# Pace of the linear steps in an AdaLN transformer block: which half's attention three MLP steps are counted to

## The chip, the cores and the metric

The kernel runs on one core of a Trainium2 chip. The metric is the device time of one execution in microseconds (us). A core has five engines that run side by side and meet through semaphores: TensorE (PE, with its weight loads as PEld), VectorE (DVE), ScalarE (ACT), GpSimd (POOL) and SyncE (SP), which here issues nearly all DMAs.

## The reference

Eight sequences of 1024 tokens with 512 features go through one transformer block whose normalisations are modulated by a condition (float32 throughout):

```python
mod = silu(condition) @ Wada + bada                  # shift, scale and gate, twice
sh_a, sc_a, gt_a, sh_m, sc_m, gt_m = split(mod, 6, axis=1)
xm = layernorm(x, g1, be1) * (1 + sc_a) + sh_a
q, k, v = split_heads(xm @ Wqkv)                     # 16 heads of 32
s = where(causal, q @ k.T * 32**-0.5, -inf)
x = x + gt_a * (softmax(s) @ v @ Wproj + bproj)
xm = layernorm(x, g2, be2) * (1 + sc_m) + sh_m
x = x + gt_m * (gelu(xm @ W1 + b1) @ W2 + b2)        # 512 -> 2048 -> 512, exact gelu
```

## The kernel before, in words

**Blocks and halves.** The work is cut into 16 blocks of 512 tokens, two to a sequence: `blocks = [(b, h)]`, `NB = 16`. Block n is a first half (h = 0, n even) or a second half (h = 1, n odd). A first half attends only to its own tokens; a second half attends to the first half's keys as well.

**Two streams on one engine.** `attend()` (L1699) walks through the attention of blocks 0 to 15 in order. `linear()` is a generator that yields before each matmul of the linear steps. Both feed TensorE, and Python decides at build time in which order their instructions are written, by a small model of when each engine is free (`now`, `written`, `left`).

**Attention.** Heads come in four groups g of four heads. A second half has four whole key tiles more per group than a first half. Each unit goes: `weights_T` (L1547) subtracts the row maxima and multiplies q and k into the PSUM tile `st`, ACT takes the exponential of the scores (L1583) into `pT`; `close` (L1754) multiplies an earlier `pT` with v (L1611); POOL adds up the weights (L1696). A first half has 10 units and so 10 exponentials, a second half 26. The row maxima come from score units (`scores`, L1477) worked out one group ahead in the same PSUM tile, of which there is one; DVE masks them (L1491) and reduces them (L1494), `split_maxima` (L1499) cuts the maximum into three bf16 parts (`mcols`, last instruction L1516), and `maxima_rows` (L1524) turns these into rows by matmuls (L1532) that ACT copies out (L1538).

**Linear steps.** The linear stream is a list of steps per window: window w is what is counted to the attention of block w. The steps are `k`, `q`, `v` (projections), `proj` (output projection), `at` and `mt` (transposes with modulation, L657), `u` (a quarter of the first MLP product with its gelu, L1031) and `d` (a part of the second MLP product), with small ones for loads, norms and gate rows. Most are written in Strassen's form: seven products on quarters of the operands. All of their matmuls are issued by the helper `matmul` (L201) at line 205. One call of it is 8 matmul instructions in the trace. A `k`, `q`, `v`, `u` step is 28 calls, and the eight MLP steps of a block (`m` = u0 to u3, d0 to d3) are 4 x 28 calls and 32, 32, 16 and 32 calls. Weights come in 256 KB pieces through a ring of nine buffers, in the order of the steps.

Window w holds, for the MLP, the steps of block n = w - 1. What doesn't fit is put into the list `late`, with which the next window begins (L256):

```python
steps = late + [("v", w), ("load_xr", n)] + rows_a + [("proj", n), ("k", w + 1)]
steps += [("mt", n), ("q", w + 1)] + rows_m + own        # own: u0, u1, u2 and loads
```

In the last attention window, w = 15, only the first late step stands ahead of the loads and the projection (L251):

```python
steps = late[:1] + [("load_xr", n)] + rows_a + [("proj", n), ("mt", n)] + late[1:]
```

**The pace.** `planned_time(w)` (L327) adds up fixed costs of a window's steps (853 ns for two calls). `exp_need` (L1782) and `score_need` (L1786) give fixed costs to the attention's units. For each block, `attend` sets a rate (L1721), and each unit adds to what is due (`pace`, L1780):

```python
stream["rate"] = planned_time(n) / mine * (0.7 if n == 0 else 1.0)
stream["due"] += ns * stream["rate"]
```

`step_aside` (L1338) runs before each attention instruction group and decides whether linear work goes first; `own` and `other` are the modelled waits of the attention and of the linear stream, and `done_linear` is what the linear stream has booked (430 ns for a call):

```python
if done_linear[0] < stream["due"]:
    if other > own + 100:
        break
elif own <= max(other, 50):
    break
work()
```

So a linear stream behind its account is worked off even where the attention is ready; one that is ahead only fills the attention's waits. Apart from that, `until(condition)` (L1334) runs linear work alone: `close` calls it until v of the block whose keys come next is done. `run_excursions(1)` (L1729) hands one waiting ACT job, such as a gelu or a norm, to ACT after each exponential, and in first halves also after each score unit; it is also called for all jobs when no linear step can go on.

Of the kernel before, what the change touches and what calls it, by code (L numbers as in the profile page):

```python
# [22 lines left out]
def kernel(  # L23
# [207 lines left out]
    def mlp_steps(n):  # L231
        return [("u", n, i) for i in range(NQ)] + [("d", n, part) for part in range(4)]
# [8 lines left out]
    late = []  # L241
    for w in range(1, NB):
        n = w - 1
        m = mlp_steps(n)
        even = blocks[n][1] == 0
        rows_a = [("rows", blocks[n][0], "a")] if even else []
        rows_m = [("rows", blocks[n][0], "m")] if even else []
        own = m[:1] + ([("load_xa", w + 2)] if w + 2 < NB else []) + m[1:3]
        own += [("norm_a", w + 2)] if w + 2 < NB else []
        if w == NB - 1:  # L250
            steps = late[:1] + [("load_xr", n)] + rows_a + [("proj", n), ("mt", n)] + late[1:]  # L251
            steps += [("v", w)] + rows_m + own + m[3:6]
            late = m[6:]
        else:

            steps = late + [("v", w), ("load_xr", n)] + rows_a + [("proj", n), ("k", w + 1)]  # L256
            if w == 1:
                steps = [("load_xr", n)] + rows_a + [("k", w + 1), ("proj", n)]
            steps += [("mt", n), ("q", w + 1)] + rows_m + own
            at = [("at", w + 2)] if w + 2 < NB else []  # L260
            if blocks[w][1] == 0:

                steps += m[3:5]
                late = m[5:6] + at + m[6:]
            else:
                steps += m[3:6] + at
                late = m[6:]
        plan[w] = steps
# [104 lines left out]
    at, r0 = [], 0  # L373
# [1497 lines left out]
```

## Time and profile before

| | |
|---|---|
| median of 3 runs | 3552.7 us (3548.19 to 3553.39) |
| profiled execution: time | 3555.04 us |
| profiled execution: span | 3553.2 us |
| mean granted TensorE clock | 0.998 |
| instructions | 123721 |
| DMA traffic | 441.76 MB, mean 124 GB/s |

The span is the time from the first to the last instruction of the profiled execution; its whole time is 1.8 us longer. In the profile, L205 is line 205 of the kernel; a group such as "bank<-w,hT" names the tile written and the tiles read. Busy times are in us, the mean of one instruction in ns, and a wait is shown with the instruction that ended it. The tiles tell the linear steps apart: `hT` stands for the d steps, `xm_m` and `t_m` for the u steps, `xm_a` and `t_a` for q, k and v.

### The profile page before, as it was taken

How to read it: one execution, taken by the hardware profiler on the slowest of the kernel's cores; microseconds unless marked ns; L12 is line 12 of the kernel's file. 1: busy time of each engine (PE TensorE's matmuls, PEld its weight loads, DVE VectorE, ACT ScalarE, POOL GpSimd, SP SyncE). 2: the span in 40 equal slices, each digit the busy share in tenths (PEclk: the TensorE clock that was granted, in tenths of full speed). 3: DMA queues.
4: the chain of work that ended last, by engine and by line, in shares of the span. 5: the costliest groups of instructions: out<-in, count | busy, mean ns of one | idle time of the engine just before them, and what ended most of it. 6: DMA issues, size and time to landing. Idle time of an engine off the chain costs nothing.

```text
span 3553.2 us, 123721 instructions
## 1 busy us (share of the span) xinstructions
PE 3486.2 (98%) x56189; PEld 1814.8 (51%) x56189; DVE 1926.9 (54%) x2106; ACT 1271.1 (36%) x1407; POOL 2066.2 (58%) x2194
## 2 busy tenths in 40 slices
PE   8999999999999999999999999999999999999999
PEld 4444555445554455545555445454554545545445
DVE  5765664644636456364464645636446464554463
ACT  2335233342333524235242342423524244241521
POOL 3675745666466663666636666466664666644650
PEclk9999999999999999999999999999999999999999
DMA  6742334334343344433434334343343433435334
GB/s 209 257 147 88 115 114 119 116 107 141 116 135 108 97 138 117 147 96 97 141 111 147 99 95 140 108 150 100 94 144 106 150 96 103 133 99 152 88 115 137
DMA packets 319944, 441.76 MB, mean 124 GB/s; under 512 B 26568, under 2 KB 188676, under 8 KB 319420
## 3 DMA queue, kind: packets, MB, share of 16 engines
q1 hardware_dynamic: 319168, 433.54, 40.4%
q8 instruction: 443, 7.26, 0.9%
q14 instruction: 81, 0.66, 0.1%
q10 hardware_dynamic: 252, 0.29, 0.0%
HBM read 404.32 MB, written 29.41 MB: 122 GB/s over the span
## 4 chain that ended last, share of the span: by engine, by line
PE 87%; DVE 5%; ACT 3%; POOL 2%; issue 1%; DMA 1%; SPq 0%; DVEq 0%; ACTq 0%; POOLq 0%
PE bank L205 60%; PE sc L1477 8%; PE po L1611 7%; PE st L1570 6%; DVE mx L1494 3%; PE st L1558 2%; PE bank L657 2%; PE bank L1632 2%; ACT pT L1583 1%; POOL pT L1696 1%; DVE sc L1491 1%; DVE hT L1089 1%; DVE xr L162 1%; ACT hT L1031 1%; PE bank L1532 0%
## 5 line engine op out<-in xcount | busy, mean ns | idle before, releaser
L1696 POOL TENSOR_TENSOR pT<-pT,pT 128x256 f32<-128x256 f32 (+3 forms) x1254 | 1200.0, 992 | 260.2 <-ACT pT L1583 165.3
L1583 ACT ACTIVATE pT<-st 128x2048 f32<-128x2048 f32 x288 | 541.0, 1878 | 1154.6 <-PE st L1570 1048.6
L205 PE MATMUL bank<-w,hT 128*32 128x256 f32 x14336 | 807.4, 380 | 0.3 <-ACT xm_a L667 0.2
L1494 DVE TENSOR_REDUCE mx<-sc 128x4 f32<-128x2048 f32 (+3 forms) x384 | 665.7, 1754 | 134.0 <-PE sc L1477 126.5
L205 PEld LDWEIGHTS bank<-w,hT 128*32 128x32 f32 x14336 | 455.2, 110 | 343.6 <-issue 49.5
L205 PE MATMUL bank<-xm_m,w 128*32 128x256 f32 x8192 | 502.1, 381 | 1.8 <-DVE u_u L197 1.7
L205 PE MATMUL bank<-t_m,w 128*32 128x256 f32 x6144 | 380.7, 380 | 0.4 <-DVE hT L197 0.3
L205 PEld LDWEIGHTS bank<-xm_m,w 128*32 128x32 f32 x8192 | 254.6, 110 | 245.1 <-issue 81.2
L1588 POOL TENSOR_SCALAR_AFFINE_SELECT pT<-pT 128x512 f32<-128x512 f32 x256 | 168.8, 677 | 344.2 <-ACT pT L1583 342.8
L1477 PE MATMUL sc<-kT,qT 32*128 32x512 f32 (+3 forms) x3072 | 329.2, 520 | 6.0 <-DVE mx L1494 2.9
L1491 DVE TENSOR_TENSOR sc<-sc,mask 128x1024 f32<-128x1024 f32 (+1 forms) x160 | 162.9, 1018 | 277.1 <-PE sc L1477 186.7
L1611 PE MATMUL po<-pT,v 128*32 128x512 f32 (+3 forms) x3072 | 305.9, 493 | 2.8 <-POOL pT L1588 2.8
L1570 PE MATMUL st<-qT,kT 32*128 32x512 f32 (+3 forms) x3072 | 300.2, 486 | 0.0
L205 PEld LDWEIGHTS bank<-t_m,w 128*32 128x32 f32 x6144 | 192.7, 110 | 168.4 <-issue 32.5
L205 PE MATMUL bank<-xm_a,w 128*32 128x256 f32 x3968 | 245.5, 381 | 0.0
L165 POOL TENSOR_TENSOR qT<-top,rec 128x512 f32<-128x512 f32 x61 | 78.2, 1282 | 274.5 <-ACT rec L1650 270.9
L1477 PEld LDWEIGHTS sc<-kT,qT 32*128 32x128 f32 x3072 | 129.7, 184 | 161.6 <-ACT pT L1583 75.3
L197 DVE TENSOR_TENSOR hT<-bank,u_u 128x512 f32<-128x512 f32 x192 | 128.4, 686 | 134.0 <-PE bank L205 131.5
L205 PE MATMUL bank<-w,qT 128*32 128x256 f32 (+1 forms) x2944 | 190.4, 399 | 0.8 <-DMA w<-in_L_cond_Wproj_dram 0.8
L1031 ACT ACTIVATE hT<-hT,cols 128x512 f32<-128x512 f32 x256 | 164.2, 711 | 54.9 <-DVE hT L197 54.3
L205 PE MATMUL bank<-t_a,w 128*32 128x256 f32 x2944 | 182.8, 380 | 0.9 <-DMA w<-kept_qkv_S 0.9
L205 PEld LDWEIGHTS bank<-xm_a,w 128*32 128x32 f32 x3968 | 125.6, 110 | 105.4 <-issue 22.5
(217 smaller groups left out, 3491.9 us busy)
## 6 DMA issues: line engine op xcount, KB each, us to landing
w<-in_L_cond_W_dram SPq DMA_DIRECT2D x384, 256.0 KB
w<-kept_up_S SPq DMA_DIRECT2D x256, 256.0 KB
w<-kept_down_S SPq DMA_DIRECT2D x256, 256.0 KB
w<-kept_qkv_S SPq DMA_DIRECT2D x180, 256.0 KB
w<-in_L_cond_Wqkv_dram SPq DMA_DIRECT2D x147, 256.0 KB
hat<-in_x_dram SPq DMA_DIRECT2D x64, 256.0 KB
xr<-in_x_dram SPq DMA_DIRECT2D x64, 256.0 KB
out_dram<-xr SPq DMA_DIRECT2D x64, 256.0 KB
```

The source lines that it names most:

```text
L165: nc.gpsimd.tensor_tensor(out, a, b, op)
L197: nc.vector.tensor_tensor(out, src, other, op)
L205: nc.tensor.matmul(ps[r, :], lhsT[:, r], rhs, start=start, stop=stop, skip_group_check=True)
L1031: nc.scalar.activation(hT[:, i, :], hT[:, i, :], AF.Gelu, bias=cols[:, O_B1 + f : O_B1 + f + 1])
L1477: nc.tensor.matmul(sc[:, j, c0 : c0 + w], qTs[n][r, gg, ts(qt, P)], keys_of(n, kh)[r, gg, :w], start=True, stop=True, skip_group_check=True,)
L1491: nc.vector.tensor_tensor(place, place, shape_of.to_broadcast(place.shape), ALU.add)
L1494: nc.vector.tensor_reduce(maxima[n, gg][:, kh, qt, :], sc[:, :, c0 : c0 + w], axis=AX.X, op=ALU.max)
L1570: nc.tensor.matmul(st[:, j, c0 : c0 + w], kT[r, gg, ts(k % NTT, P)], qT[r, gg, TB - w :], start=False, stop=True, skip_group_check=True,)
L1583: nc.scalar.activation(pT[:, :, :used], st[:, :, :used], AF.Exp, scale=scale)
L1588: nc.gpsimd.affine_select(diagonal, diagonal, pattern=[[0, HPG], [1, P]], compare_op=ALU.is_ge, fill=0.0, base=0, channel_multiplier=-1,)
L1611: nc.tensor.matmul(po[r, TB - w :], v[:, k % NTT, g * P + j * hd : g * P + (j + 1) * hd], pT[:, j, c0 : c0 + w], start=(k == 0), stop=last ...
L1696: nc.gpsimd.tensor_tensor(into, into, pT[:, j, c0 : c0 + w], ALU.add)
```

## The change

For a window w that is a first half, the lists before and after are:

```diff
             at = [("at", w + 2)] if w + 2 < NB else []
             if blocks[w][1] == 0:
 
-                steps += m[3:5]
-                late = m[5:6] + at + m[6:]
+                late = m[3:6] + at + m[6:]
             else:
                 steps += m[3:6] + at
                 late = m[6:]
```

Before, u3 and d0 end the list of a first half's window and d1 opens that of the second half's. After, u3, d0 and d1 all open that of the second half's. This concerns the first halves 2, 4, ..., 14 and the second halves 3, 5, ..., 15 behind them. The order of the linear stream stays the same except in window 15, where `late[:1]` is u3 instead of d1, so that `load_xr`, the gate rows, `proj` and `mt` of block 14 come between u3 and d0 instead of between d1 and d2. No instruction's work is added or taken away.

## The prediction

> **What bounds the kernel now.** I read the page first. It gives the span, TensorE's (PE) busy time and the number of exponentials.
>
> ```profile
> span 3553.2 us, 123721 instructions
> ...
> PE 3486.2 (98%) x56189; PEld 1814.8 (51%) x56189; DVE 1926.9 (54%) x2106; ACT 1271.1 (36%) x1407; POOL 2066.2 (58%) x2194
> ...
> L1583 ACT ACTIVATE pT<-st 128x2048 f32<-128x2048 f32 x288 | 541.0, 1878 | 1154.6 <-PE st L1570 1048.6
> ```
>
> PE is idle for 3553.2 - 3486.2 = 67.0 us, and no other engine is near its limit. The change adds no instruction, so its worth is what it does to those 67 us. The 288 exponentials are 8 x (10 + 26): a first half has 10 units, a second half 26. Counting them in the timeline gives each attention's stretch ("window n" runs from the first exponential of half n to that of the next). The busy time by windows, for 4 and 12 (first halves) and 5 and 13 (second halves): start:end, length, PE busy (instructions), then PEld, DVE, ACT, POOL, clock, DMA.
>
> ```profile
> 807.50:982.70 175.20, 175.00 (x2932) 95.56 (x2928) 101.52 (x114) 55.01 (x67) 92.48 (x109) 1.00 0.43 128
> 982.70:1242.50 259.80, 256.13 (x4036) 129.87 (x4032) 130.20 (x138) 103.15 (x108) 170.87 (x169) 1.00 0.38 114
> ...
> 2553.60:2722.00 168.40, 166.56 (x2773) 89.93 (x2769) 96.14 (x107) 51.41 (x62) 90.57 (x109) 1.00 0.42 124
> 2722.00:2991.70 269.70, 265.85 (x4212) 135.47 (x4208) 133.88 (x146) 108.88 (x116) 169.18 (x170) 1.00 0.38 116
> ```
>
> Idle PE is 0.2 and 3.7 us in windows 4 and 5, 1.8 and 3.9 us in 12 and 13. The list of waits says on what: the first row is window 12's, the second stands in window 5's answer and, digit for digit, in 13's.
>
> ```profile
> PE bank L1532 <- POOL mcols L1516: 1.5, 1, 1.5
> ...
> PE st L1558 <- DVE mx L1494: 3.1, 4, 1.1
> ```
>
> **The change, part by part.** Outside window 15 the order of the linear steps stays the same: what leaves a first half's list leads the next one. Only the rates differ. By the code's own costs a first half needs 65.2 us (exponentials 15.0, scores 50.2) and a second half 100.6 us. The planned linear time goes from 131.4 to 105.8 us and from 162.1 to 187.7 us: (14 + 16) x 853 ns = 25.6 us move, u3 and d0. The third step named, d1, was counted late already. The rates go from 2.02 to 1.62 and from 1.61 to 1.87.
>
> The rate acts only where the linear account is behind what is due. Elsewhere linear work just fills the wait for the score tile, and at v(w), which every attention needs early, it runs alone until v is done (a burst). So I counted the linear matmuls (line 205) by stretch; 8 instructions are one call. The rows are: the last but one and the last unit of window 4; the last of 12; the last two of 14; the first five units of 5; the burst in 5; that in 13; three units of 13 with one score group each; two units of 15 with none.
>
> ```profile
> 928.30:958.10 29.80, 22.54 (x396) 12.43 (x400) 1.00 0.47 143
> 958.10:982.70 24.60, 18.97 (x340) 10.55 (x336) 1.00 0.40 113
> ...
> 2702.80:2722.00 19.20, 13.56 (x237) 7.16 (x233) 1.00 0.29 86
> 3114.90:3140.80 25.90, 18.66 (x324) 10.08 (x328) 1.00 0.35 104
> 3140.80:3157.80 17.00, 11.36 (x196) 5.84 (x192) 1.00 0.33 94
> ...
> 982.70:1025.80 43.10, 29.47 (x516) 15.87 (x512) 1.00 0.35 101
> ...
> 1025.80:1067.70 41.90, 37.53 (x688) 21.99 (x680) 1.00 0.58 181
> 2765.50:2816.80 51.30, 46.97 (x864) 27.72 (x856) 1.00 0.56 174
> ...
> 2899.70:2925.10 25.40, 16.52 (x285) 8.98 (x289) 1.00 0.42 136
> 3157.80:3167.30 9.50, 4.69 (x84) 2.36 (x80) 1.00 0.27 79
> ```
>
> The last unit has 42.5 calls in window 4, 29.6 in 12 and 24.5 in 14. It shrinks because the account books 430 ns for a call that the plan counts at 426.5; over the 672 calls of a pair of windows that is 2.4 us. I take 24.5 as what the score tile's waits absorb unforced, so by window 14 the account holds almost nothing. With 25.6 us (60 calls) less due, every first half falls to that level: window 4 gives up (340 - 196 + 396 - 324) / 8 = 27 calls, window 12 gives up 5, window 14 none. In the next second half the account is then ahead, so its first five units fall from 64.5 calls to the unforced (285 + 84) / 8 = 46, 18 fewer. The burst makes up for both: in window 5 from 86 calls to 86 + 27 + 18 = 131, in window 13 from 108 to 108 + 5 + 18 = 131. From there the linear position, the attention unit and who waits for whom are as before, and at the end of the second half the sums due are equal.
>
> So 18 to 45 calls move later by some tens of us, in seven pairs of windows. They cost nothing themselves if PE stays full in the longer burst. Its cover is the linear stream alone: 48 calls in 20.93 us (0.43 us each) without an idle entry (fourth row of the next timeline). Its DMA share is 0.56 at 174 GB/s, so pieces have room. SP's queue keeps its order; POOL and DVE have fewer attention instructions in a burst.
>
> What can cost is a PE wait in the stretches that lose calls. The timelines show one: TensorE's rows of maxima (line 1532) behind POOL's split. First window 4, then window 12, the same place.
>
> ```profile
> 811.08 6.25 PE L205 MATMUL bank<-w,hT 128*32 128x256 f32 x112
> ...
> 821.56 0.41 PE L1532 MATMUL bank<-ident_b,mcols 128*32 128x128 bf16 x16
> ...
> 2557.19 4.09 PE L205 MATMUL bank<-w,hT 128*32 128x256 f32 x72
> ...
> 2564.05 0.41 PE L1532 MATMUL bank<-ident_b,mcols 128*32 128x128 bf16 x16 [1.52 <-POOL mcols L1516]
> ```
>
> With 14 calls and more after the scores nothing is late; with the unforced 9 PE stands for 1.52 us, and the linear calls and the row's copy on ACT stand behind it. In windows 4, 6 and 8 the account still forces the longer fill; at the lower rate (10.8 us due in that unit become 8.7) it does so no more. I take 3 x 1.5 = 4.5 us, with ends 0 and 4.5.
>
> The second halves have the same rows just before the burst. In window 13:
>
> ```profile
> 2757.82 6.25 PE L205 MATMUL bank<-w,hT 128*32 128x256 f32 x112
> ...
> 2765.25 2.80 PE L205 MATMUL bank<-w,hT 128*32 128x256 f32 x48
> 2767.86 0.41 PE L1532 MATMUL bank<-ident_b,mcols 128*32 128x128 bf16 x16
> ...
> 2780.32 20.93 PE L205 MATMUL bank<-w,hT 128*32 128x256 f32 x384
> ```
>
> And the split on POOL, in window 13 and in window 12, with DVE's instruction beside the latter:
>
> ```profile
> 2762.54 0.25 POOL L1515 CAST mcols<-rest 128x16 bf16<-128x16 f32 x1
> 2762.87 0.27 POOL L1516 TENSOR_TENSOR mcols<-rest,mcols 128x16 bf16<-128x16 f32 x1
> ...
> 2561.70 1.15 POOL L1515 CAST mcols<-rest 128x16 bf16<-128x16 f32 x1
> 2562.93 1.07 POOL L1516 TENSOR_TENSOR mcols<-rest,mcols 128x16 bf16<-128x16 f32 x1
> ...
> 2561.52 2.35 DVE L1089 TENSOR_TENSOR hT<-hT,hT 128x1024 f32<-128x1024 f32 x2
> ```
>
> The split ends at 2763.14, and the rows start 4.7 us later, after 14 + 6 = 20 calls. Some 9 to 11 calls fewer take 3.9 to 4.8 us: no wait, or 0.1. I take 0.2 us x 7 = 1.4 us; the ends are 0 and window 12's 1.5 each, 0 to 10.5.
>
> In window 12 the two POOL instructions took 2.2 us instead of 0.5, within a DVE subtraction that reads two SBUF tiles. The Trainium skill ("SBUF — State Buffer", section "SBUF: two separate sides") says that such a DVE operation and a POOL operation that reads SBUF hold one port pair in turn, exclusively; these rows agree. By it the split is quick or slow as the first subtraction of a d step meets it or not, which speaks against moving d0 there.
>
> In window 15 the order does change: `late[:1]` is u3 instead of d1, so load_xr(14), proj(14) and mt(14) come before d0 and d1, with load_xr's four DMAs and the gate rows' two. proj follows load_xr directly in both, and mt waits for v(15) in both: 0, from -1 to +2 us.
>
> The sum is 4.5 + 1.4 = 5.9 us. The profiled execution took 3555.0 us, span 3553.2 and 1.8 around it; it would take 3560.9. It stands 2.3 us above the median of the runs, 3552.7, on which I put the forecast: **3558.6 us**.
>
> **The rivals.**
>
> *Slower by a late gelu.* d1 needs u3's gelu, which is handed out one per exponential. Until window 15, 7028 + 5248 u instructions are 54.80 steps of 224:
>
> ```profile
> L205 PE MATMUL bank<-xm_m,w 128*32 128x256 f32 x7028 | 432.4, 381 | 1.8 <-DVE u_u L197 1.7
> ...
> L205 PE MATMUL bank<-t_m,w 128*32 128x256 f32 x5248 | 325.4, 380 | 0.4 <-DVE hT L197 0.3
> ```
>
> So 33.5 calls are left to u3's end at that unforced level, 34 to 39 with d0's interleaved, and the sixth exponential comes at call 46. The margin is some 7 calls, 3 us. If it is missed, the gelu is issued inside the burst, behind the copy that ends d0. These are the table load, gelu and copy of window 13:
>
> ```profile
> 2755.26 1.28 ACT L1031 ACT_TABLE_LOAD   x1
> 2756.55 2.56 ACT L1031 ACTIVATE hT<-hT,cols 128x512 f32<-128x512 f32 x4
> 2762.84 0.58 ACT L192 COPY p_d<-bank 128x512 f32<-128x512 f32 x1 [3.73 <-PE bank L205]
> ```
>
> PE would stand for 0.58 + 1.28 + 2.56 = 4.4 us. Near the end of the kernel a PE wait of 2.2 us is in a stretch with a clock of 0.94, which is 0.06 x 30 = 1.8 us lost:
>
> ```profile
> 3400.00:3430.00 30.00, 27.77 (x452) 13.87 (x448) 24.46 (x23) 6.38 (x9) 26.89 (x20) 0.94 0.37 116
> ...
> PE po L1611 <- POOL pT L1588: 2.2, 1, 2.2
> ```
>
> That gives 7 x (4.4 + 1.8) + 4.5 = 48 us, 3601. Chance 0.11. The Trainium skill ("TensorE: Matmul & The Clock Gate", "What's actually happening") lets the clock fall after an idle window of about 3.4 us; here 2.2 us sufficed, and 1.5 us did not (clock 1.00 in window 12). By the page the clock's part would come just the same at 4.4 us.
>
> *Slower by the rows.* If the slow split of window 12 meets the second halves' rows, 1.7 us are added to the 0.1: with a wait of 1.8 us each and the clock's 1.8 us, 7 x 3.6 + 4.5 = 30 us, 3582. It decides once the split ends 4.7 us or less after the scores' reduction than now, as fewer calls leave no slack. For it: both have the same form. Against: d0's subtraction is issued two units earlier. Chance 0.13.
>
> *Faster.* More linear work per unit could fill the 3.1 us that PE waits for DVE's maxima in a second half: 7 x 3.1 = 22 us, 3531. Against: these waits lie behind the burst, where the account is ahead, and are the same with bursts of 86 and 108 calls. Chance 0.13.
>
> *The change hardly does what it says.* Bursts reset the position and no wait appears: 3553, give or take 2. Chance 0.17.
>
> **How the numbers follow.** My forecast has 0.46, with its own range 3552 to 3566 from the ends of its terms. 0.2% is 7.1 us (3545.6 to 3559.8), about what a measurement can tell from no change. Of the forecast 0.28 lies inside, 0.18 above; of the faster rival 0.02 inside. Faster: 0.11. Same: 0.28 + 0.17 + 0.02 = 0.47. Slower: 0.18 + 0.11 + 0.13 = 0.42. The range 3543 to 3584 takes in the rows' rival and leaves out the late gelu and most of the faster case.
>
> **What would show it.** Right: first halves shorter (window 4 by about 12 us) and second halves longer by as much; bursts of about 131 calls in all second halves; a 1.5 us wait of line 1532 also in windows 4, 6 and 8; the 3.1 us unchanged. Wrong: a wait in the burst on line 1031 or 1516 above 2 us, with a clock below 1.00; or first halves as long as before.

## The result, and the profile after

| | before | after |
|---|---|---|
| median (6 runs each) | 3553.05 us (3548.19 to 3555.15) | 3527.26 us (3523.56 to 3531.16) |
| span of the profiled execution | 3553.2 us | 3524.9 us |
| idle PE (span less PE busy) | 67.0 us | 42.7 us |

The ratio is 0.9929, with a 95% interval of 0.9916 to 0.9942: 25.8 us or 0.71% faster. The forecast was 3558.6 us, so even the sign was wrong. The page after, its span, its engines and the exponentials:

```profile
span 3524.9 us, 123741 instructions
...
PE 3482.2 (99%) x56189; PEld 1800.1 (51%) x56189; DVE 1882.3 (53%) x2086; ACT 1286.5 (36%) x1422; POOL 2065.1 (59%) x2205
...
L1582 ACT ACTIVATE pT<-st 128x2048 f32<-128x2048 f32 x288 | 541.1, 1879 | 1046.0 <-PE st L1569 933.0
```

PE does the same 56189 matmuls and the same 288 exponentials follow. Of the 28.3 us that the span lost, 24.3 are idle time of PE and 4.0 its busy time. Over the twelve profiles of this case PE's busy time for these matmuls varies from 3479.3 to 3486.5 us, so the 4.0 us can't be told from chance. (The new kernel is one line shorter: its L1493 is the old L1494, its L1557 the old L1558.) Windows 4, 5, 12 and 13 after, with the columns that they had before:

```profile
797.70:964.50 166.80, 166.47 (x2772) 89.92 (x2768) 93.79 (x102) 54.14 (x65) 89.39 (x107) 1.00 0.41 126
964.50:1227.50 263.00, 262.99 (x4166) 133.61 (x4161) 130.31 (x149) 107.25 (x113) 170.38 (x171) 1.00 0.38 117
2522.80:2696.40 173.60, 172.95 (x2892) 93.77 (x2888) 94.80 (x103) 54.12 (x65) 89.53 (x109) 1.00 0.42 127
2696.40:2956.40 260.00, 259.25 (x4092) 129.97 (x4088) 130.28 (x149) 107.22 (x113) 169.85 (x170) 1.00 0.39 115
```

Window 5 had 3.7 us of idle PE and has none; window 13 had 3.9 and has 0.8. The pair 4 and 5 takes 429.8 us instead of 435.0, the pair 12 and 13 takes 433.6 instead of 438.1. From PE's list of waits (engine, tile, line, what ended the wait: total us, times, longest), first before, then after:

```profile
PE st L1558 <- DVE mx L1494: 19.1, 25, 1.1
PE bank L1532 <- POOL mcols L1516: 7.1, 6, 1.6
```

```profile
PE bank L1531 <- POOL mcols L1515: 5.1, 7, 1.6
...
PE st L1557 <- DVE mx L1493: 1.1, 2, 0.9
```

One wait explains most of it: `weights_T` waiting for DVE's maxima falls from 19.1 us in 25 waits to 1.1 us in 2. It is the 3.1 us per second half that the prediction had listed and declared unchanged; in the trace before it stands in the second halves 3 to 13 (2.4 us in window 3) and not in 15. 18.0 of the 24.3 us are this wait; the rest is spread over the maxima rows (2.0 us) and several small ones.

### The profile page after: what moved, and what is told of

Read it like the earlier page. It is cut to its first block, busy times and chain, and to the rows that moved or that the text cites. A ratio compares the mean times of both kernels' runs of the same rounds, so it can differ in the third digit from the quotient of the medians.

```text
span 3524.9 us, 123741 instructions
## 1 busy us (share of the span) xinstructions
PE 3482.2 (99%) x56189; PEld 1800.1 (51%) x56189; DVE 1882.3 (53%) x2086; ACT 1286.5 (36%) x1422; POOL 2065.1 (59%) x2205
## 4 chain that ended last, share of the span: by engine, by line
PE 93%; DVE 2%; POOL 2%; DMA 1%; issue 1%; ACT 1%; SPq 0%; DVEq 0%; POOLq 0%; ACTq 0%
PE bank L205 64%; PE sc L1476 9%; PE po L1610 7%; PE st L1569 7%; PE st L1557 2%; PE bank L656 2%; DVE mx L1493 2%; PE bank L1631 2%; POOL pT L1695 1%; PE bank L1531 0%; POOL hT L165 0%; DVE sc L1490 0%; DMA w<-in_L_cond_Wada_dram 0%; DMA hat<-in_x_dram 0%; DMA w<-in_L_cond_Wproj_dram 0%
## 5 line engine op out<-in xcount | busy, mean ns | idle before, releaser
L1695 POOL TENSOR_TENSOR pT<-pT,pT 128x256 f32<-128x256 f32 (+3 forms) x1254 | 1179.0, 975 | 202.0 <-ACT pT L1582 115.8
L205 PE MATMUL bank<-w,hT 128*32 128x256 f32 x14336 | 797.5, 379 | 0.1
L1493 DVE TENSOR_REDUCE mx<-sc 128x4 f32<-128x2048 f32 (+3 forms) x384 | 665.9, 1755 | 133.8 <-PE sc L1476 127.1
```

The costliest lines, as they stand in the source:

```text
L205: nc.tensor.matmul(ps[r, :], lhsT[:, r], rhs, start=start, stop=stop, skip_group_check=True)
L1493: nc.vector.tensor_reduce(maxima[n, gg][:, kh, qt, :], sc[:, :, c0 : c0 + w], axis=AX.X, op=ALU.max)
L1695: nc.gpsimd.tensor_tensor(into, into, pT[:, j, c0 : c0 + w], ALU.add)
```

## The experiments

**What they had to tell apart.** The new trace shows all that was moved, and beyond it that the attention behind the burst runs otherwise. Three theories say why. ORDER: the new order in window 15 does it. FILL: with more linear work due per unit of a second half there is more to fill the waits, the more the better. PHASE: u3's gelu now comes last before the burst; the planner's model thereby enters the attention behind the burst in another state, and places work differently from there on (a phase is the pattern in which that placement then repeats). ADDS is a finer form of PHASE: what counts is where the planner then puts the adds `xr += row_gba`.

PHASE came from three places in the trace. First ACT around window 5's burst, after:

```profile
999.00 1.88 ACT L1582 ACTIVATE pT<-st 128x2048 f32<-128x2048 f32 x1 [8.92 <-PE st L1569]
1000.90 1.28 ACT L1030 ACT_TABLE_LOAD   x1
1002.19 2.56 ACT L1030 ACTIVATE hT<-hT,cols 128x512 f32<-128x512 f32 x4
...
1052.28 1.28 ACT L145 ACT_TABLE_LOAD   x1
1062.01 1.88 ACT L1582 ACTIVATE pT<-st 128x2048 f32<-128x2048 f32 x1 [8.44 <-PE st L1569]
```

The gelu takes the slot behind the sixth exponential (999.00), as predicted, and the table of the exponentials is loaded again inside the burst, 8.4 us ahead of the next exponential, where it costs nothing. But the model in `note_act` doesn't know of that early load: at the first exponential after a gelu it books a constant, `TABLE` = 1283 ns, on top. Before the change the last of the gelus and exponentials ahead of the burst was an exponential, and nothing was booked. In the model ACT and so the attention are now 1.3 us later, and more linear work goes in front. PE behind the same burst, before and after:

```profile
1068.37 0.61 PE L205 MATMUL bank<-w,qT 128*32 128x256 f32 x8
1068.81 1.04 PE L205 MATMUL bank<-w,t 128*32 128x256 f32 x16
1069.78 1.14 PE L1477 MATMUL sc<-kT,qT 32*128 32x512 f32 x8
```

```profile
1062.68 0.61 PE L205 MATMUL bank<-w,qT 128*32 128x256 f32 x8
1063.12 1.91 PE L205 MATMUL bank<-w,t 128*32 128x256 f32 x32
1064.84 0.61 PE L205 MATMUL bank<-w,qT 128*32 128x256 f32 x8
1065.39 1.14 PE L1476 MATMUL sc<-kT,qT 32*128 32x512 f32 x8
```

Six calls of linear work ahead of the scores instead of three (8 instructions are one call). From here on the two schedules differ in who does what. Third, DVE some 20 us later, before, and then PE's waits in the same stretch:

```profile
1091.45 5.03 DVE L162 TENSOR_TENSOR xr<-xr,row_gba 128x512 f32<-128x512 f32 x3
1096.40 2.28 DVE L1494 TENSOR_REDUCE mx<-sc 128x4 f32<-128x2048 f32 x1
...
1115.77 0.68 DVE L569 BATCH_NORM_STATS2 st_m<-xr 128x6 f32<-128x512 f32 x1
...
1217.32 4.45 DVE L1089 TENSOR_TENSOR hT<-hT 128x1024 f32<-128x1024 f32 x2
```

```profile
1098.73 0.40 PE L1558 MATMUL st<-mrow,minus_ones 32*128 32x512 bf16 x4 [0.69 <-DVE mx L1494]
...
1123.89 0.40 PE L1558 MATMUL st<-mrow,minus_ones 32*128 32x384 bf16 x8 [1.09 <-DVE mx L1494]
...
1130.85 0.40 PE L1558 MATMUL st<-mrow,minus_ones 32*128 32x512 bf16 x4 [0.61 <-DVE mx L1494]
...
1225.36 0.40 PE L1558 MATMUL st<-mrow,minus_ones 32*128 32x512 bf16 x4 [0.72 <-DVE mx L1494]
```

These are the 3.1 us. Three adds (5.03 us) stand on DVE ahead of a reduction, and PE waits 0.69 us for it. The norm's statistics, which need those adds, are done only after 1116, so that the transposes (L657, in the new kernel L656), which stand in these places after, come too late for the two waits in the middle; this link is read from the order of the rows. The last wait stands behind two subtractions of d0 (4.45 us). The same place after, on POOL and on DVE:

```profile
1084.90 4.26 POOL L165 TENSOR_TENSOR xr<-xr,row_gba 128x512 f32<-128x512 f32 x3
```

```profile
1084.85 0.69 DVE L162 TENSOR_TENSOR xr<-xr,row_gba 128x512 f32<-128x512 f32 x1 [2.40 <-POOL xr L165]
1085.46 2.28 DVE L1493 TENSOR_REDUCE mx<-sc 128x4 f32<-128x2048 f32 x1
...
1093.48 0.68 DVE L568 BATCH_NORM_STATS2 st_m<-xr 128x6 f32<-128x512 f32 x1
```

Three of the four adds are on POOL, DVE's reduction starts 0.6 us after the one that is left, the statistics end at 1094, and window 5 has no wait of PE at all. The kernel's function `either` makes this choice from the modelled clocks of the two engines: an add goes to DVE only where the model has it end there more than 1500 ns sooner than on POOL. All second halves from 3 to 13 look like window 5: three adds on DVE before, one after.

In all experiments the arithmetic is complete; they change only when work is due, what the planner books, or which engine does an add.

**Only the rate** (before, with the planned time of 60 calls, 30 of the code's units of two, moved from each first half's window to the next; lists and order as before):

```diff
-        return parts + sum(costs.get(step[0], 0) for step in plan[w])
+        moved = 30 * MM
+        shift = 0 if w < 2 else moved if w % 2 else -moved
+        return shift + parts + sum(costs.get(step[0], 0) for step in plan[w])
```

> The kernel before with its lists and its order; planned_time alone is shifted by 30 x 853 ns from each first half (from 2 on) to the second half behind it. Three theories. PHASE: the longer lone stretch of linear work now begins right after u3's gelu, so the planner's model charges ACT's table reload (1.28 us) to the first exponential behind it; PE then fills three calls more before the next scores, and from there the residual adds fall to POOL instead of DVE and no scores' reduction waits behind them. FILL: the higher rate of the second halves puts more linear work into each unit. ORDER: the gain comes from the other order of steps in window 15. PHASE and FILL: as the changed kernel, 3527 us (3520 to 3534), PE's wait for DVE's maxima about 1 us in all instead of 19.1. ORDER: 3553.

It took 3526.97 us (3526.09 to 3530.81), ratio 0.9931 (0.9918 to 0.9945): the whole gain.

**Only the order in window 15** (the new lists for w = 14 alone; `shift` is added to the planned time, so that the rates of windows 14 and 15 are those of before):

```diff
-                steps += m[3:5]
-                late = m[5:6] + at + m[6:]
+                steps += m[3:5] if w < NB - 2 else []
+                late = (m[5:6] if w < NB - 2 else m[3:6]) + at + m[6:]
...
+        shift = {NB - 2: 30 * MM, NB - 1: -30 * MM}.get(w, 0)
```

> The kernel before with the changed order of window 15 alone (u3 ahead of the loads and proj of block 14); planned_time of windows 14 and 15 is corrected so that all rates are those of before. PHASE and FILL: 3553 us within 4, the wait for DVE's maxima still about 19 us. ORDER: 3527 to 3540.

3553.04 us (3552.27 to 3556.07), ratio 1.0001 (0.9992 to 1.0009). ORDER has fallen; this edit is worth nothing, as predicted.

**Twice the rate** (as the first experiment, with 120 calls moved):

```diff
-        moved = 30 * MM
+        moved = 60 * MM
```

> The kernel before with planned_time shifted twice as far as in the change, 60 x 853 ns (51 us) from each first half to the second half behind it. PHASE: the first halves stand already at their unforced level, u3's gelu stays ahead of the lone stretch, so 3527 within 4. FILL: still more due per unit in the second halves, so as fast as 3527 or faster by up to 10 us, with the longest unforced units longer.

3531.45 us (3527.63 to 3533.83), ratio 0.9936 (0.9924 to 0.9949). Twice the shift brings no more; the time is even just above what PHASE allowed (3531), with an interval that overlaps that of the single shift. FILL wants a gain that grows with the rate; PHASE has a switch that is on or off.

**The booking alone, in before.** Nothing of the change is in this kernel. In the second halves 3 to 13 the planner books `TABLE` at the first exponential behind the burst, as it does after the change:

```diff
-        note_act(170 + 3.34 * used, "exp", ["st"], [("p", slot)])
+        after_burst = h == 1 and g == 0 and parts[0][0] == NTT + 2 and 3 <= n < NB - 1
+        note_act(170 + 3.34 * used + after_burst * TABLE, "exp", ["st"], [("p", slot)])
```

> The kernel before; the model alone books 1283 ns more for one exponential, the first behind the lone stretch, in the second halves 3 to 13. No instruction is added, rates and lists are those of before. PHASE: PE's wait for DVE's maxima falls from 19.1 us to 1 to 6, and the time by 13 to 18 us to 3535 to 3540. FILL and ORDER: 3553 within 4, and the wait stays.

3525.31 us (3523.82 to 3526.98), ratio 0.9921 (0.9908 to 0.9935). More than expected: 1283 ns that exist only on paper, booked in six places, give the whole gain without a step being moved. PE behind window 5's burst now has the new kernel's order, six calls and then the scores:

```profile
1065.15 0.61 PE L205 MATMUL bank<-w,qT 128*32 128x256 f32 x8
1065.58 1.91 PE L205 MATMUL bank<-w,t 128*32 128x256 f32 x32
1067.31 0.61 PE L205 MATMUL bank<-w,qT 128*32 128x256 f32 x8
1067.86 1.14 PE L1477 MATMUL sc<-kT,qT 32*128 32x512 f32 x8
```

**The booking taken out of after.** The whole change, but the model takes the table as loaded at the same exponentials:

```diff
+        if h == 1 and g == 0 and parts[0][0] == NTT + 2 and 3 <= n < NB - 1:
+            table[0] = "exp"
         note_act(170 + 3.34 * used, "exp", ["st"], [("p", slot)])
```

> The changed kernel; the model alone does not book the table reload (1283 ns) at the first exponential behind the lone stretch in the second halves 3 to 13 (the reload itself stays). PHASE: PE's wait for DVE's maxima comes back, 13 to 19 us in all, and the time is 3540 to 3546. FILL and ORDER: 3527 within 4, the wait about 1 us.

3556.49 us (3553.99 to 3559.86), ratio 1.001 (1.0001 to 1.0019). The gain is gone and the old wait is back, more of both than expected; from the list of waits:

```profile
PE st L1557 <- DVE mx L1493: 19.8, 26, 1.1
PE bank L1531 <- POOL mcols L1515: 11.7, 12, 1.6
```

Behind the bursts of the second halves 3 to 13 three calls precede the scores again, and three of the four adds stand on DVE. Up to the bursts it is the changed kernel. So it is also what the prediction had in mind: the steps counted to the second halves, and the attention placed as before. The maxima rows then wait 4.6 us longer than before the change (11.7 against 7.1), and the time is 3.1 us above that of before (by the interval of the ratio, 0.4 to 6.8). The predicted terms were 5.9 us.

**A smaller booking** (430 ns, one call, instead of 1283):

```diff
-        note_act(170 + 3.34 * used + after_burst * TABLE, "exp", ["st"], [("p", slot)])
+        note_act(170 + 3.34 * used + after_burst * 430, "exp", ["st"], [("p", slot)])
```

> The kernel before; the model books 430 ns (one call) instead of 1283 ns (three calls) more for the first exponential behind the lone stretch in the second halves 3 to 13. PHASE with any shift enough: 3527 within 4. PHASE with a threshold (the three calls are needed for the adds to change engines): 3553 within 4, the wait about 19 us.

3554.73 us (3552.54 to 3559.91), ratio 1.0005 (0.9996 to 1.0014), and 21.8 us of waits for the maxima. It is a switch: 430 ns don't throw it, 1283 do. With 430 ns four calls instead of three precede the scores behind each burst, but three adds stay on DVE.

**The booking in window 1 as well** (`n < NB - 1` without `3 <= n`):

```diff
-        after_burst = h == 1 and g == 0 and parts[0][0] == NTT + 2 and 3 <= n < NB - 1
+        after_burst = h == 1 and g == 0 and parts[0][0] == NTT + 2 and n < NB - 1
```

> The kernel before; the model books 1283 ns more for the same exponential in all second halves 1 to 13, so in window 1 too, where PE's waits are 3.5 us. PHASE: as the same kernel without window 1 (3525) or up to 3 us faster, 3522 to 3526.

3528.86 us (3524.39 to 3529.19), ratio 0.9934 (0.9921 to 0.9948). The seventh place adds nothing; the time lies above the 3522 to 3526 expected, and the intervals of this kernel, of the booking alone and of after overlap.

**The adds to POOL, in before.** No booking, no moved step; `xr += row_gba` goes to POOL in the 14 blocks that pass through this line, 56 of the 64 adds (the planner goes on choosing for the 8 others):

```diff
-            xt_job = lambda t=t: add_to(
-                residual[n][:, t, :], gate_rows["gba"], [("row", "gba")], [("xr", n, t)]
-            )
+            def xt_job(t=t):
+                xt = residual[n][:, t, :]
+                keys = [("row", "gba"), ("xr", n, t)], [("xr", n, t)]
+                nc.gpsimd.tensor_tensor(xt, xt, gate_rows["gba"], ALU.add)
+                note("POOL", 120 + 2.28 * D, *keys)
```

> The kernel before; the four adds of the gated bias to the residual (xr += row_gba) in each projected block are always given to POOL, none to DVE. The earlier shift is shown to be worth 28 us; open is by which link. ADDS: the adds on DVE hold up one scores' reduction and, through the late norm, the transposes that would fill PE later; then the wait for DVE's maxima falls from 19.1 to about 5 us and the time to 3536 to 3542. FIRST WAIT ONLY: only the wait directly behind the adds goes (0.7 us in each of six second halves): 3549. WHOLE PHASE: the adds are a by-product and the wait stays near 19 us: 3553 within 3.

3529.07 us (3527.96 to 3533.40), ratio 0.9933 (0.9921 to 0.9945): 7 us below what ADDS allowed. In this schedule the adds on DVE carry the loss. The list of waits has

```profile
PE st L1561 <- DVE mx L1497: 8.6, 14, 0.9
```

By windows, this wait fell from 17.9 to 3.9 us in the second halves 3 to 13, and 3.5 us of it are new, in first halves. The gain of 24 us is larger than that wait alone: idle PE fell by 19.0 us in all (3527.3 - 3479.3 = 48.0), 4.6 of them at the maxima rows, and busy PE by 6.9. The order behind window 5's burst is still the old one, three calls and then the scores:

```profile
1063.96 0.61 PE L205 MATMUL bank<-w,qT 128*32 128x256 f32 x8
1064.39 1.05 PE L205 MATMUL bank<-w,t 128*32 128x256 f32 x16
1065.37 1.14 PE L1480 MATMUL sc<-kT,qT 32*128 32x512 f32 x8
```

So the six calls are not needed for the gain; where the adds stand, with what the planner then places behind them, is enough.

**The adds to DVE, in after** (the same with `nc.vector` and `note("DVE", 60 + 1.24 * D, *keys, port=True)`):

```diff
+                nc.vector.tensor_tensor(xt, xt, gate_rows["gba"], ALU.add)
+                note("DVE", 60 + 1.24 * D, *keys, port=True)
```

> The changed kernel; the same four adds are always given to DVE. ADDS: most of the wait for DVE's maxima comes back, 12 us or more, 3540 to 3546. FIRST WAIT ONLY: 4 to 5 us, 3531 to 3533. WHOLE PHASE: 3527 within 3.

3542.41 us (3537.86 to 3543.61), ratio 0.9966 (0.9952 to 0.9979): about 15 us of the gain lost. The time is the one that ADDS gave, but not by its wait:

```profile
PE bank L205 <- ACT rec L1644: 9.9, 6, 1.6
...
PE st L1560 <- DVE mx L1496: 7.5, 8, 1.0
```

ADDS wanted 12 us or more of the second row. The schedule is another one, too: in the second halves 3 to 13 an exponential is again the last function ahead of the burst, three calls precede the scores, and the adds stand elsewhere and take 0.68 us each. So this run does not tell what adds on DVE cost in the new phase.

**The adds to POOL, in after** (the edit of before's kernel, on after). If adds on DVE are what costs, this one keeps or betters after's time:

```diff
+                nc.gpsimd.tensor_tensor(xt, xt, gate_rows["gba"], ALU.add)
+                note("POOL", 120 + 2.28 * D, *keys)
```

> The changed kernel; the four adds of the gated bias are always given to POOL, as in the run that did this to the kernel before. If the placement of the adds is the whole gain, nothing more comes: 3527 within 4. If it is one of two independent gains, 3515 to 3522.

3542.72 us (3540.20 to 3546.30), ratio 0.9974 (0.9965 to 0.9984). Both expectations were wrong: it is 15 us slower than after, as slow as with these adds on DVE, although the six calls behind the bursts stay. In its list of waits these grew (1.6, 1.1 and nothing in after):

```profile
PE sc L1479 <- ACT pT L1585: 5.5, 6, 1.6
PE st L1560 <- DVE mx L1496: 5.4, 10, 0.9
...
PE bank L205 <- ACT p_u L192: 4.6, 6, 0.8
```

So ADDS is not a rule of its own. Three adds in a row on DVE ahead of a reduction are the cost in the old phase; in the new phase 13 adds stand on DVE, one to a half, and forcing them over sets off other delays. The groups of this add on DVE (count, busy us, mean ns), of before, after and after without booking, show the two phases:

```profile
L162 DVE TENSOR_TENSOR xr<-xr,row_gba 128x512 f32<-128x512 f32 x27 | 37.4, 1423 | 19.3 <-POOL xr L165 19.1
```

```profile
L162 DVE TENSOR_TENSOR xr<-xr,row_gba 128x512 f32<-128x512 f32 x13 | 9.0, 694 | 33.5 <-POOL xr L165 33.5
```

```profile
L162 DVE TENSOR_TENSOR xr<-xr,row_gba 128x512 f32<-128x512 f32 x25 | 35.1, 1440 | 19.3 <-POOL xr L165 19.1
```

All nine kernels in which the planner chooses fall into these two kinds: 13 to 15 adds on DVE with a mean of 0.7 to 0.8 us, and 3525 to 3532 us, or 25 to 27 adds with a mean of 1.4 to 1.5 us, and 3553 to 3557 us. Nothing lies between.

**What stays open.** Why the adds forced to POOL cost 15 us in the new phase is only seen as a mixture of small waits; no run moves the adds to DVE and leaves the rest of that phase as it is. And which comparison in the planner is the first to turn over at 1283 ns and not at 430 was not traced.

## Why the prediction was wrong, point by point

**What held.** PE bounds the kernel and only its 67 us of idle time could change. Linear calls (line 205, 8 instructions each) moved from first halves into the burst. Window 4, the first five units of window 5, and its burst, after:

```profile
797.70:964.50 166.80, 121.30 (x2144) 67.08 (x2136) 1.00 0.41 126
964.50:999.00 34.50, 20.76 (x356) 11.29 (x360) 1.00 0.29 86
999.00:1062.00 63.00, 58.65 (x1080) 34.66 (x1072) 1.00 0.56 172
```

The five units have 356 / 8 = 44.5 calls, where 46 were predicted, and the burst has 135, where 131 were. In the bursts of windows 7 to 13 it is 137. Window 4 is 8.4 us shorter (predicted 12); window 5 is only 3.2 us longer, where as much was predicted. The gelu made the slot behind the sixth exponential, so the late gelu did not happen, and PE stays full in the longer burst. The order in window 15 costs 0.

**The step that failed** is the sentence "From there the linear position, the attention unit and who waits for whom are as before". The position was right, the rest wrong: the wait for DVE's maxima, which that sentence kept at 19.1 us, fell to 1.1. The prediction traced where u3's gelu goes on the chip and what a missed slot would cost, but not that the planner is a party too: its model books the return at the next exponential, where the chip has already done it, and three calls more go ahead of the scores. From there on the model chooses otherwise between DVE and POOL: 13 of these adds on DVE instead of 27. In a kernel whose schedule is written by a model, "as before" needs the model's state to be the same, not only the chip's.

**The faster rival** had the right wait. Its price, 7 x 3.1 = 22 us and 3531, is near the 25.8 us and 3527.26 in part by luck: the wait stood in six second halves, 17.9 us, and the rest of the gain is other. It got a chance of 0.13, and its reason (more linear work per unit to fill the wait) is not the one: twice the rate brings nothing more, and the booking brings all of it at the old rates. The argument against it, that the waits were the same with bursts of 86 and 108 calls, said only that the wait does not depend on the burst's length. In all those windows the last ACT function ahead of the burst was an exponential, so the sample held constant just what the change turned over.

**The cost terms.** The 4.5 us for line 1532 in windows 4, 6 and 8 did not come; in windows 10, 12 and 14, where the wait stood before, it is gone too, and the list went from 7.1 to 5.1 us. In the second halves the rows wait 2.5 us in all, where 1.4 were predicted. A term was left out here, as far as the windows show: second halves that end sooner leave the next first half less far ahead in the stream. Window 12, predicted to give up 5 calls, took on (2264 - 2149) / 8 = 14; the after row is the first of these, the before row the second:

```profile
2522.80:2696.40 173.60, 128.12 (x2264) 71.19 (x2264) 1.00 0.42 127
```

```profile
2553.60:2722.00 168.40, 121.49 (x2149) 67.54 (x2153) 1.00 0.42 124
```

With the attention placed as before (the booking taken out of after) the rows did cost: +4.6 us in the list (2.0 in windows 6 and 8, 2.5 in second halves), and 3.1 us in the time. Window 4 is 11.1 us shorter there and window 5 is 12.5 longer, as predicted. So the sign and the rough size of the 5.9 us were right for the kernel that the prediction imagined, and it was the wrong kernel.

**The range** (3543 to 3584) left out most of the faster case because that case's chance was put at 0.13. What the profile could not give was its mechanism; what it did give, 19.1 us of one wait that recurs with the same 3.1 us in the second halves shown, is the sign of a schedule caught in one repeating pattern. A change to what the planner sees ahead of it can break such a pattern (1283 ns did, 430 ns did not), and that deserved a larger chance.

## What to carry to other kernels

Where the instruction order is written by a cost model, follow an edit through the model's state (which table it believes loaded, what it books and when), not only through the chip's; a booking of 1.3 us for a load that costs nothing there was worth 28 us here. A wait that recurs identically in every period belongs to one repeating schedule and can vanish or appear as a whole, so give that its own rival. Test for it by moving the booking alone, in both directions: it costs one line and separates "more work to fill with" from "another schedule".

## What the runs showed of the hardware

The same add of two 128x512 f32 tiles on DVE took 0.69 us in after, each of the 13 times. In before, the 18 in the second halves 3 to 13 took 1.73 us each. In window 5 they ran beside POOL's sums of `pT`, and those were slowed as well: the sums of 128x512 alone (their mean in ns is the number behind the comma), first before (1091 to 1097 us), then after (1089 to 1102 us), where DVE had no operation on two SBUF tiles meanwhile:

```profile
L1696 POOL TENSOR_TENSOR pT<-pT,pT 128x512 f32<-128x512 f32 x4 | 6.8, 1728 | 0.0
```

```profile
L1695 POOL TENSOR_TENSOR pT<-pT,pT 128x512 f32<-128x512 f32 x8 | 9.9, 1268 | 0.0
```

That is 1.73 us a sum against 1.27, and 1.73 an add against 0.69. Where DVE starts first, POOL alone pays: in window 5 of after DVE's one add starts 0.05 us ahead of POOL's first and takes its 0.69 us, while POOL's takes 1.79 and the next two 1.27. The Trainium skill ("SBUF — State Buffer", section "SBUF: two separate sides") has DVE operations with two SBUF inputs and POOL operations that read SBUF hold one shared port pair in turn; these rows agree, and in both directions. It makes adds on DVE dear just where POOL is busy, which is where the old schedule put them.
